# Sturm sweeps of an eigenvalue search: one product of double width and one sum a step on GpSimd in place of three VectorE operations

## The chip, the cores and the metric

The kernel runs on one core of a Trainium2 chip. The metric is the time of one execution on the device in microseconds; lower is better. Several executions are run and their median is given. Besides, one execution is recorded by the hardware profiler; the profile and the trace are of that one.

A core has TensorE (PE: matrix products, with PEld for its weight loads), VectorE (DVE), ScalarE (ACT), GpSimd (POOL) and SyncE (SP, which issues transfers here). Each engine carries out its own queue of instructions in the order in which they were written; the engines wait for each other through semaphores.

## The reference

The program is a network of four graph layers on an input of 128 batches x 64 nodes x 256 features, with an adjacency matrix of 64 x 64. Each layer normalises its input, applies a graph operation and adds the result:

- Layer 0: two graph products with `adj`, then LSTMs over windows of 1, 2, 3 and 4 nodes, whose last states replace nodes.
- Layer 1: a product with a Laplacian that is scaled by the largest eigenvalue, then attention and a two-stage network with normalisations.
- Layer 2: graph attention.
- Layer 3: a product with the eigenvectors of a normalised Laplacian, a small network, and the product back:

```python
L_norm = d_inv_sqrt[:, None] * L * d_inv_sqrt[None, :]
_, U = jnp.linalg.eigh(L_norm)
agg = jnp.einsum('mn,bnd->bmd', U.T, features)
```

So the kernel has to decompose one symmetric 64 x 64 matrix into eigenvalues and eigenvectors. The result is needed only in layer 3, but it is a long chain of small operations.

## The kernel before, in words

**The tiling.** The rows (batch and node) are cut into 64 tiles of 128. Layer 0 works on eight groups of eight tiles; layers 1 to 3 work on sixteen groups of four. Layer 0 is mostly matrix products of 128 x 256 outputs on TensorE, with sigmoids and tanhs on ScalarE and the gate products on VectorE. Some products of windows are made by sums of pieces beforehand, and these sums and the small steps of the normalisations are on GpSimd.

**The eigenvalue search** (`eig_decomp`, line 347) runs beside layer 0. It (1) brings the matrix to tridiagonal form by 62 reflections, (2) finds all 64 eigenvalues by nine sweeps, (3) finds the vectors of the tridiagonal matrix, and (4) puts vectors of degenerate values right and hands the matrices `Ub` and `UTb` to layer 3. All of its small tiles lie in one tile named `arena`, which becomes part of the pool of working buffers once the search is over.

**A sweep** (the loop over `s_`, line 634) tests seven points in the interval of each eigenvalue. Each of 64 partitions holds one eigenvalue, and three variants of the matrix are treated at once, so an operation of the recurrence has 64 partitions x 21 columns. With `D` the diagonal, `E2` the squared couplings and `x` the points, the recurrence is p(k+1) = (D(k) - x) p(k) - E2(k-1) p(k-1), and the number of changes of sign along k tells how many eigenvalues lie below x. `DX` holds D - x for all k, `PL` the values p, and `SG` their signs. For each k, VectorE makes two products and a difference. After every eight steps the last two p are divided by the larger of their sizes, in four VectorE operations: the reduction, a lower bound, the reciprocal, the product. This happens seven times a sweep. At the end of a sweep the signs are compared, the changes are summed over k, and the intervals are shortened eightfold.

**The order of work** is computed when the program is built, by a planner (class `Plan`). Every operation is recorded with what it depends on; `schedule` then writes all queues down, in the order in which a model of the engines would start the operations. It charges each operation a duration by `cost` (line 176), for example

```python
else:
    c = 0.075 + 0.00105 * n          # VectorE, n columns
...
c = 0.44 + 0.14 * n if op.kw.get("op") is ALU.pow else 0.12 + 0.00218 * n   # GpSimd
return c, c + 0.05
```

The second value is the time after which another operation may use the result. The planner lets two kinds of operations never overlap: those of GpSimd, and those of VectorE whose operands all lie in SBUF (`op.port`; reductions and the statistics of normalisations are excepted). Where both could start at one time, VectorE goes first. The search is the group `EIG`: on TensorE its operations go ahead of all others, and on all other engines they go behind all others that could start at that time (`rank`, line 328). On the chip, an engine then waits at the head of its queue for whatever that instruction needs, also where the plan had it ready.

Of the kernel before, what the change touches and what calls it, by code (L numbers as in the profile page):

```python
# [8 lines left out]
ALU = mybir.AluOpType  # L9
# [3 lines left out]
N = 64  # L13
KS = 7
# [332 lines left out]
def eig_decomp(plan, room, adj, adjT, ident, idf, ones):  # L347
# [13 lines left out]
    V, G, PE, ACT, SP = (plan.proxy(e) for e in ("V", "G", "PE", "ACT", "SP"))  # L361
# [3 lines left out]
    def scope():  # L365
        inner.reset([0])
        return inner

    def T(shape, name):
        return room.tile(shape)  # L370

    def W(shape, name, bufs=None):

        if bufs is None:
            bufs = 2 if shape[-1] < N or name == "lab" else 1
        ring = kept.setdefault((name, tuple(shape)), [])
        if len(ring) < bufs:
            ring.append(room.tile(shape))
        else:
            ring.append(ring.pop(0))  # L380
        return ring[-1]
# [56 lines left out]
    ph = scope()  # L438
# [4 lines left out]
    for k in range(N - 2):  # L443
# [17 lines left out]
        s = W([N, 1], 's')  # L461
# [21 lines left out]
        p = pf[:N, :2 * N]  # L483
# [43 lines left out]
    M = N - 1  # L527
# [68 lines left out]
    E2 = T([N, 3, N], 'E2')  # L596
# [30 lines left out]
    V.tensor_copy(lo, l1.to_broadcast([N, 3]))  # L627
    C = 3 * KS
    ph = scope()
    PL = ph.tile([N, N + 1, C])  # L630
    V.memset(PL[:, 0, :], 1.0)
    DX = ph.tile([N, N, 3, KS])
    SG = ph.tile([N, N + 1, C])
    for s_ in range(NSWEEP):
        V.tensor_scalar(w, w, 1.0 / (KS + 1), None, op0=ALU.mult)
        x = W([N, 3, KS], 'x')
        V.tensor_scalar(x, c['ramp'], w, None, op0=ALU.mult)
        V.tensor_add(x, x, lo.unsqueeze(2).to_broadcast([N, 3, KS]))
        for l in range(3):
            V.tensor_mul(DX[:, :, l, :], BM[:, l, :].unsqueeze(2).to_broadcast([N, N, KS]), x[:, l, :].unsqueeze(1).to_broadcast([N, N, KS]))  # L640
            V.tensor_sub(DX[:, :, l, :], DM[:, l, :].unsqueeze(2).to_broadcast([N, N, KS]), DX[:, :, l, :])
        DXf = DX.rearrange('p k l s -> p k (l s)')
        for k in range(N):
            V.tensor_mul(PL[:, k + 1, :], DXf[:, k, :], PL[:, k, :])
            if k:
                b = W([N, 3, KS], 'b', 2)
                V.tensor_mul(b, PL[:, k - 1, :].rearrange('p (l s) -> p l s', l=3), E2[:, :, k - 1:k].to_broadcast([N, 3, KS]))
                V.tensor_sub(PL[:, k + 1, :], PL[:, k + 1, :], b.rearrange('p l s -> p (l s)'))
            if k % 8 == 7 and k < N - 1:
                mm = W([N, C], 'mm')  # L650
                V.tensor_reduce(mm, PL[:, k:k + 2, :].rearrange('p k c -> p c k'), op=ALU.max, axis=AX.X, apply_absolute_value=True)
                V.tensor_scalar(mm, mm, 1e-30, None, op0=ALU.max)
                V.reciprocal(mm, mm)
                V.tensor_mul(PL[:, k:k + 2, :], PL[:, k:k + 2, :], mm.unsqueeze(1).to_broadcast([N, 2, C]))
        V.tensor_scalar(SG, PL, 0.0, None, op0=ALU.is_lt)
        NE = DXf
        V.tensor_tensor(NE, SG[:, 1:, :], SG[:, :N, :], op=ALU.not_equal)
        ct = W([N, 3, KS], 'ct')
        V.tensor_reduce(ct.rearrange('p l s -> p (l s)'), NE.rearrange('p k c -> p c k'), op=ALU.add, axis=AX.X)
        V.tensor_tensor(ct, ct, li.unsqueeze(2).to_broadcast([N, 3, KS]), op=ALU.is_le)  # L660
        sm = W([N, 3], 'sm')
        V.reduce_sum(sm, ct, axis=AX.X)
        V.scalar_tensor_tensor(lo, sm, w, lo, op0=ALU.mult, op1=ALU.add)
# [7 lines left out]
    ph = scope()  # L671
# [80 lines left out]
    def one(name):  # L752
        return W([N, 1], name)
# [7 lines left out]
    for l in (1, 0):  # L761
# [10 lines left out]
        b = one('bc')  # L772
# [11 lines left out]
        t = W([N, N], 't64')  # L784
# [3 lines left out]
        t = W([N, N], 't64')  # L788
# [23 lines left out]
        t = W([N, N], 't64')  # L812
# [120 lines left out]
def gnn_kernel(ctx: ExitStack, tc: tile.TileContext, a, out):  # L933
# [213 lines left out]


    QT, Vc, inner = eig_decomp(plan, room, adj2[:N], adjT2[:N], ident[:N, :N], ident, ones)
    for dst, lhs, rhs in ((Ublk, QT, Vc), (UTblk, Vc, QT)):  # L1150
        l2 = inner.tile([P, 2, N])
# [560 lines left out]
```

## Time and profile before

| what | us |
|---|---|
| median of three runs | 2153.46 (2152.71 to 2155.54) |
| the profiled execution | 2151.09 |
| its span, first to last instruction | 2149.3 |
| TensorE busy | 2102.0 |
| VectorE busy | 1796.7 |
| ScalarE busy | 1124.1 |
| GpSimd busy | 708.4 |
| tridiagonal form and all before it, from the start to | 538 |
| nine sweeps, from and to | 538 to 1178 |
| vectors, from and to | 1178 to 1348 |

The times of the stages are read from the trace: the sweeps begin with the first operations of 64 x 448 and end with the last reduction of 64 x 1344 columns. Almost every instruction stands under line 344, where the planner issues them, so the groups are told apart by the tile names and by the shapes: `arena` is the search, `mids` and `bank` and `big` are the layers. A row of a group gives its count, after the bar its busy time in us and its mean in ns, and then the idle time of the engine before it with what ended it. A row of a timeline gives the start and the length in us. Busy times are of one profiled execution.

### The profile page before, as it was taken

The numbers are of one execution on the slowest core, as the hardware profiler recorded it, in microseconds if no ns is written. First come the engines' busy times: TensorE is split into PE (matmuls) and PEld (weight loads), VectorE is DVE, ScalarE is ACT, GpSimd is POOL, SyncE is SP. The second block draws the span as 40 slices with busy tenths as digits, with TensorE's granted clock in tenths as the row PEclk, the third lists the DMA queues.
The fourth block names the chain that finished last, engine by engine and source line by source line (L and its number), as shares of the span: only waits on it lengthen the run. The fifth ranks groups of instructions, "written<-read, shape, count | busy, mean of one in ns | idle before, by whom it ended". The sixth has DMA issues, their size and how long they took to land.

```text
span 2149.3 us, 46200 instructions
## 1 busy us (share of the span) xinstructions
PE 2102.0 (98%) x16772; PEld 1665.0 (77%) x16772; DVE 1796.7 (84%) x7434; ACT 1124.1 (52%) x2465; POOL 708.4 (33%) x1040
## 2 busy tenths in 40 slices
PE   9999999999999999999999999999999999999998
PEld 6688688688778778778778788877777877887776
DVE  5788888888999999989989898767787789876787
ACT  3354354355345345345345444566667666665783
POOL 7211211310110110110110002696556657864353
PEclk9999999999999999999999999999999999999999
DMA  5000100100100100100000111200000100000001
GB/s 206 1 3 22 42 2 22 41 1 21 40 1 21 40 1 21 40 1 21 26 1 21 50 40 51 90 1 2 21 22 21 41 22 21 11 12 11 2 2 60
DMA packets 44868, 57.70 MB, mean 27 GB/s; under 512 B 8928, under 2 KB 38496, under 8 KB 44640
## 3 DMA queue, kind: packets, MB, share of 16 engines
q1 hardware_dynamic: 43536, 53.71, 7.6%
q8 instruction: 131, 2.15, 0.4%
q10 hardware_dynamic: 1104, 1.05, 0.2%
q14 instruction: 97, 0.79, 0.1%
HBM read 37.53 MB, written 16.78 MB: 25 GB/s over the span
## 4 chain that ended last, share of the span: by engine, by line
PE 79%; DVE 11%; POOL 3%; issue 3%; ACT 2%; DMA 2%; SPq 0%; DVEq 0%; ACTq 0%; POOLq 0%
PE bank L344 79%; DVE stat L344 3%; DVE arena L344 3%; DVE big L344 3%; POOL stat L344 2%; DVE mids L344 1%; DVE sums L344 1%; DMA big<-in_x_dram 1%; ACT big L344 1%; ACT mids L344 1%; POOL arena L344 0%; ACT arena L344 0%; POOL big L344 0%; DVE Whh L344 0%; SPq L344 0%
## 5 line engine op out<-in xcount | busy, mean ns | idle before, releaser
L344 PE MATMUL bank<-big,Wih 128*128 128x256 f32 (+3 forms) x2408 | 731.7, 426 | 14.7 <-DVE arena L344 6.9
L344 PEld LDWEIGHTS bank<-big,Wih 128*128 128x128 f32 x2408 | 440.3, 190 | 183.0 <-issue 100.2
L344 ACT ACTIVATE mids<-bank,bl 128x256 f32<-128x256 f32 (+3 forms) x528 | 274.8, 527 | 385.7 <-PE bank L344 383.3
L344 PE MATMUL bank<-big,Whh 128*128 128x256 f32 (+2 forms) x1692 | 448.0, 366 | 1.5 <-DVE big L344 1.4
L344 DVE TENSOR_TENSOR arena<-arena 64x21 f32<-64x21 f32 (+5 forms) x2253 | 372.3, 195 | 29.5 <-POOL arena L344 1.2
L344 PEld LDWEIGHTS bank<-big,Whh 128*128 128x128 f32 x1692 | 306.8, 190 | 40.6 <-issue 8.6
L344 PE MATMUL bank<-big,sums 128*128 128x168 f32 (+2 forms) x1472 | 263.8, 321 | 1.6 <-ACT big L344 1.5
L344 POOL TENSOR_SCALAR stat<-stat 128x4 f32<-128x4 f32 (+1 forms) x228 | 69.8, 307 | 514.0 <-DVE stat L344 499.2
L344 PEld LDWEIGHTS bank<-big,sums 128*128 128x128 f32 (+1 forms) x1472 | 220.5, 185 | 17.4 <-issue 3.4
L344 ACT COPY mids<-bank 128x168 f32<-128x168 f32 (+2 forms) x427 | 146.2, 364 | 151.9 <-PE bank L344 146.0
L344 DVE TENSOR_TENSOR big<-mids 128x512 f32<-128x512 f32 (+2 forms) x256 | 141.5, 562 | 33.9 <-ACT mids L344 30.7
L344 ACT ACTIVATE mids<-mids,bl 128x336 f32<-128x336 f32 (+3 forms) x192 | 102.1, 539 | 78.7 <-DVE mids L344 74.9
L344 DVE TENSOR_TENSOR mids<-bank,mids 128x168 f32<-128x168 f32 (+2 forms) x322 | 116.1, 368 | 25.1 <-PE bank L344 17.6
L344 DVE SCALAR_TENSOR_TENSOR arena<-arena 64x1 f32<-64x1 f32 (+15 forms) x565 | 124.3, 243 | 6.1 <-POOL arena L344 2.5
L344 POOL TENSOR_TENSOR stat<-stat,mhalf 128x4 f32<-128x4 f32 (+1 forms) x114 | 123.9, 1088 | 5.6
L344 ACT ACTIVATE mids<-big 128x256 f32<-128x256 f32 (+2 forms) x176 | 89.4, 510 | 62.7 <-DVE big L344 46.3
L344 POOL TENSOR_TENSOR big<-big 128x168 f32<-128x168 f32 (+1 forms) x30 | 21.4, 726 | 272.5 <-DVE arena L344 105.7
L344 DVE TENSOR_SCALAR arena<-arena 64x1 f32<-64x1 f32 (+8 forms) x533 | 102.4, 199 | 8.3 <-POOL arena L344 0.4
L344 DVE TENSOR_TENSOR big<-big,mids 128x256 f32<-128x256 f32 (+2 forms) x194 | 95.2, 492 | 9.7 <-ACT mids L344 8.5
L344 PE MATMUL bank<-Wih,big 128*128 128x256 f32 x384 | 94.1, 383 | 3.1 <-DVE big L344 0.9
L344 POOL TENSOR_TENSOR arena<-arena 64x1 f32<-64x1 f32 (+1 forms) x70 | 46.8, 669 | 145.9 <-ACT arena L344 105.8
L344 ACT ACT_TABLE_LOAD x55 | 70.6, 1283 | 35.9 <-PE bank L344 18.0
(371 smaller groups left out, 3747.9 us busy)
## 6 DMA issues: line engine op xcount, KB each, us to landing
big<-in_x_dram SPq DMA_DIRECT2D x30, 512.0 KB, 5.5
put<-big SPq DMA_DIRECT2D x16, 512.0 KB, 2.8
arena<-put SPq DMA_DIRECT2D x8, 512.0 KB, 6.6
out_dram<-arena SPq DMA_DIRECT2D x16, 256.0 KB, 2.3
Wih<-in_WihT_dram SPq DMA_DIRECT2D x3, 1024.0 KB, 11.9
Whh<-in_WhhT_dram SPq DMA_DIRECT2D x3, 1024.0 KB, 13.9
big<-put SPq DMA_DIRECT2D x5, 512.0 KB, 5.4
out_dram<-big SPq DMA_DIRECT2D x10, 256.0 KB, 2.2
```

Source lines behind the costliest of these rows:

```text
L344: getattr(self.engines[op.eng], name)(*map(real, args), **{k: real(a) for k, a in kw.items()})
```

## The change

Each step of the recurrence becomes two GpSimd operations. The coefficients are laid out as pairs, `CO[:, k] = (-E2(k-1), D(k) - x)`, so that one product of 42 columns with the pair (p(k-1), p(k)) makes both terms, and one sum of 21 columns makes p(k+1). The negated couplings are written once, ahead of the sweeps. The first step has one product and stays on VectorE. The row of ones at the head of `PL` is set by GpSimd in each sweep, because the signs now overwrite `PL` and the tile `SG` is gone. The rescale after every eight steps stays on VectorE, with its four operations.

```diff
     PL = ph.tile([N, N + 1, C])
-    V.memset(PL[:, 0, :], 1.0)
-    DX = ph.tile([N, N, 3, KS])
-    SG = ph.tile([N, N + 1, C])
+    CO = ph.tile([N, N, 2, C])
+    l3 = lambda t: t.rearrange('p k (l s) -> p k l s', l=3)
+    DX = l3(CO[:, :, 1, :])
+    for l in range(3):
+        V.tensor_scalar(l3(CO[:, 1:, 0, :])[:, :, l, :], E2[:, l, :M].unsqueeze(2).to_broadcast([N, M, KS]), -1.0, None, op0=ALU.mult)
     for s_ in range(NSWEEP):
...
-        DXf = DX.rearrange('p k l s -> p k (l s)')
-        for k in range(N):
-            V.tensor_mul(PL[:, k + 1, :], DXf[:, k, :], PL[:, k, :])
-            if k:
-                b = W([N, 3, KS], 'b', 2)
-                V.tensor_mul(b, PL[:, k - 1, :].rearrange('p (l s) -> p l s', l=3), E2[:, :, k - 1:k].to_broadcast([N, 3, KS]))
-                V.tensor_sub(PL[:, k + 1, :], PL[:, k + 1, :], b.rearrange('p l s -> p (l s)'))
+        G.memset(PL[:, 0, :], 1.0)
+        V.tensor_mul(PL[:, 1, :], CO[:, 0, 1, :], PL[:, 0, :])
+        for k in range(1, N):
+            b = W([N, 2, C], 'b', 2)
+            G.tensor_tensor(b, PL[:, k - 1:k + 1, :], CO[:, k], op=ALU.mult)
+            G.tensor_tensor(PL[:, k + 1, :], b[:, 0, :], b[:, 1, :], op=ALU.add)
             if k % 8 == 7 and k < N - 1:
...
-        V.tensor_scalar(SG, PL, 0.0, None, op0=ALU.is_lt)
-        NE = DXf
-        V.tensor_tensor(NE, SG[:, 1:, :], SG[:, :N, :], op=ALU.not_equal)
+        V.tensor_scalar(PL, PL, 0.0, None, op0=ALU.is_lt)
+        NE = CO[:, :, 1, :]
+        V.tensor_tensor(NE, PL[:, 1:, :], PL[:, :N, :], op=ALU.not_equal)
```

## The prediction

> **What bounds the kernel now.** I read the page from the top: the span and the busy shares, the 40 slices, then the chain.
>
> ```profile
> span 2149.3 us, 46200 instructions
> PE 2102.0 (98%) x16772; PEld 1665.0 (77%) x16772; DVE 1796.7 (84%) x7434; ACT 1124.1 (52%) x2465; POOL 708.4 (33%) x1040
> PE   9999999999999999999999999999999999999998
> POOL 7211211310110110110110002696556657864353
> PE 79%; DVE 11%; POOL 3%; issue 3%; ACT 2%; DMA 2%; SPq 0%; DVEq 0%; ACTq 0%; POOLq 0%
> ```
>
> TensorE bounds it: busy 2102 of 2149.3 us, in every slice, with 79% of the chain. At most 47 us can be won by taking waits away. GpSimd is nearly empty where the sweeps are. The timeline of VectorE shows the first sweep's operations from 538 us and the last count at 1175 to 1178 us, so nine sweeps take 640 us, 71 each. The sums of that stretch:
>
> ```profile
> 538.00:1178.00 640.00, 633.70 (x3819) 497.86 (x3818) 588.83 (x2697) 285.72 (x647) 67.13 (x96) 1.00 0.06 20
> ```
>
> The columns are the length, then busy PE, weight loads, DVE, ACT and POOL. TensorE idles 6.3 us of 640: the LSTM's matmuls fill it while VectorE, 92% busy, does their elementwise work and the sweeps in between. The sweeps are background work; relief of VectorE alone can win about those 6.3 us, plus some of the 6.2 us in the 170 after.
>
> The groups of that stretch show what goes and what the new owner does for its operations:
>
> ```profile
> L344 DVE TENSOR_TENSOR arena<-arena 64x21 f32<-64x21 f32 x1726 | 241.8, 178 | 17.0
> L344 POOL TENSOR_TENSOR big<-big,big 128x168 f32<-128x168 f32 x24 | 13.8, 606 | 4.0 <-DVE arena L344 3.1 <-DVE big L344 0.8
> L344 POOL TENSOR_SCALAR stat<-stat 128x4 f32<-128x4 f32 x16 | 5.8, 363 | 340.2 <-DVE stat L344 339.2
> ```
>
> GpSimd's timeline in one normalisation shows short operations that depend on each other, and VectorE's one rescale:
>
> ```profile
> 728.06 0.23 POOL L344 TENSOR_SCALAR stat<-stat 128x4 f32<-128x4 f32 x1 [96.30 <-DVE stat L344]
> 728.37 1.04 POOL L344 TENSOR_TENSOR stat<-stat,mhalf 128x4 f32<-128x4 f32 x1
> ...
> 732.34 0.21 POOL L344 TENSOR_TENSOR stat<-stat 128x4 f32<-128x4 f32 x1
> 732.64 0.23 POOL L344 TENSOR_SCALAR stat<-stat 128x4 f32<-128x4 f32 x1
> ```
>
> ```profile
> 546.90 0.19 DVE L344 TENSOR_REDUCE arena<-arena 64x21 f32<-64x42 f32 x1
> 547.13 0.17 DVE L344 TENSOR_SCALAR arena<-arena 64x21 f32<-64x21 f32 x1
> 547.33 0.28 DVE L344 RECIPROCAL arena<-arena 64x21 f32<-64x21 f32 x1
> 547.65 0.91 DVE L344 TENSOR_TENSOR arena<-arena 64x42 f32<-64x42 f32 x6
> ```
>
> A GpSimd product of 4 columns takes 0.21 us, and the next dependent one starts 0.08 to 0.09 us after its end (728.29 to 728.37, 732.55 to 732.64). On VectorE eight 21-wide operations in a row took 1.20 us (from 545.67), 0.15 each.
>
> **What the Trainium skill says.** GPSIMD Engine Reference, section 3.1: a two-input elementwise operation costs GpSimd about 2.6 cycles an element against VectorE's 1. The trace agrees: 128x4 to 128x168 is 0.21 to 0.61 us, 2.4 ns a column. SBUF — State Buffer, section "Who interferes with whom": a VectorE operation with two SBUF inputs and a GpSimd operation that reads SBUF exclude each other for the whole instruction. It agrees: the 128x4 scalar operation, 230 ns at its shortest, has a mean of 363 in this stretch, where such VectorE work, its groups added up, is 82% of the time. Perfetto Trace Analysis, section "GPSIMD Engine Instruction": time GpSimd by the spacing of starts; I do, with the gaps.
>
> **What the change removes, adds and moves.** Each sweep loses 64+126-1 = 189 VectorE operations of 21 columns, 1701 in all: 238 us of 178 ns that overlap in part. Each gains 63 GpSimd products of 42 columns and 63 sums of 21, 1134 in all. The negated couplings (three 441-column operations once, about 0.4 us each by the 64x448 row's 622 ns) and the sign test in place are worth about 1 us on VectorE, hidden under TensorE's 98%; uncovered they cost that 1 us. The nine GpSimd memsets, about 0.1 us each, come at a sweep's start; VectorE's first product waits for them, and what is queued behind it is LSTM products. No DMA moves. What matters is that the recurrence crosses to another engine and back at seven rescales a sweep, in queues whose order is fixed beforehand.
>
> That order is computed with the planner's charges (its cost function). It charges GpSimd 0.12 + 0.00218n us, with 0.05 more of latency, of which 0.04 count on the same engine: 0.212 + 0.166 + 0.08 = 0.457 us a step. The chip's, an estimate: 42 columns 0.28 us and 21 columns 0.24 us, by the 0.208 at 4 columns and the single 128x32 sum's 252 ns, and 0.08 behind each: **0.68 us a step**. Nothing in the trace shows these shapes on 64 partitions, so I bound the step: 0.50 (no gap, 0.26 + 0.24) to 0.95 (every operation met by the lock at the 363/230 ratio, 0.82, and a crossing more).
>
> One sweep on the chip: 63 x 0.68 = 42.8; seven rescales, 0.96 us from 546.90 to 547.86 and two crossings of 0.1, 8.1; ends (sign test, count, new points: 604.53 to 618.98 in the trace) 14.4; GpSimd's other work in its queue, 67.1 us in 640, 6.8 in 65; the lock, 133 ns at 82% share, so 39 ns at the 24% that the LSTM alone has (155 us of such products in 640, its groups added up), times 126, 5.0. Sum 77.1, times nine **694 us**.
>
> One sweep in the written order: 63 x 0.457 = 28.8; rescales by its charges 7 x 1.1 = 7.7; ends 14.4. It lets VectorE's SBUF work and GpSimd never overlap, and VectorE wins ties. The other such work is charged 189 us in 640, 30% (311 VectorE operations 132, 96 GpSimd ones 57), so the chain's 28.8 to 36.5 us stretch by 1/0.7: 12 to 16 more. Sum 63.2 to 66.5, nine **569 to 599 us**; I take 590. TensorE's work beside the sweeps is thus only 590 us worth.
>
> The difference is 104 us. Where it goes: the reduction of each rescale stands in VectorE's in-order queue and waits for GpSimd. Behind it stand the LSTM's gate products, for them ACT's tanh waits, and TensorE's next step for the hidden state. Slack in that chain absorbs a lag once, some us, not 72 times; blocks of eight steps that fit badly add about as much. Finishing the search earlier in TensorE's terms may give back 3 of the 6 us idle after 1178. So 2149.3 + 101 = 2250; the median of the runs stands 4.2 above the profiled span (its execution took 2151.1), so **2254 us**.
>
> **Rivals.**
> Likeliest, chance 0.60: GpSimd's chain paces the sweeps, 2195 to 2320, for steps of about 0.58 to 0.78 us.
> Fits in, 0.12 (0.09 faster): the step costs no more than the order gives it, 0.68 - (694 - 590)/567 = 0.50 us, the lower bound. TensorE then stays the bound and VectorE's relief takes away the waits in and after the sweeps: 2153.5 - 12 = 2142. For it: the planner's charge for 512 columns (1.24 us) meets the 1.15 to 1.33 of the rows, and spans of GpSimd are rough. Against: the gaps are starts less ends, seen at each dependent pair. It decides at 0.50 us a step.
> Half absorbed, 0.13: TensorE's queue has enough ready work to swallow half of each lag: 2204. For it, eight banks and two groups under way; against, one in-order VectorE queue for both.
> Locked harder, 0.15: each GpSimd operation waits for whole products of the LSTM, 0.4 to 0.7 us long, and they for it: 0.14 us in place of 0.04 for 126 x 9 operations, 113 more: 2367. For it, 1.05 us for a 0.23 us operation among the 16; against, most are at 0.23.
> That the work doesn't move is no case: the calls name the engine.
>
> **How the numbers follow.** The range 2170 to 2345 holds the first case, the half-absorbed one and about half of the hard lock; it leaves out the faster end and the far tail. About 0.2% is what a measurement of this kernel can tell from no change. Faster 0.09, same 0.03, slower 0.88.
>
> **What would show it.** TensorE's idle time between the first and last sweep rises from 6 to about 100 us, in gaps ended by VectorE's or ACT's products; VectorE idles before 64x42 reductions with GpSimd as releaser, 63 times, some 1 to 2 us each; the sweeps last near 690 us; GpSimd gains about 300 us busy, VectorE loses 240. If a step's start-to-start is near 0.5 us, or TensorE's idle time stays under 20 us, the prediction is wrong; if a step is near 0.9 us, the lock is larger than I take it.

## The result, and the profile after

The changed kernel takes **2203.4 us** (median of four runs, 2201.9 to 2207.3) against 2153.5 before: 1.0233 times the time, 95% interval 1.0219 to 1.0247. It is 50 us slower. The forecast was slower by 100 us, 2254, with a range of 2170 to 2345. The direction and the mechanism were right, the size was twice too large.

The page of the changed kernel: span, busy shares, and the slices of TensorE, VectorE and GpSimd.

```profile
span 2201.2 us, 45704 instructions
PE 2122.2 (96%) x16772; PEld 1668.6 (76%) x16772; DVE 1595.9 (73%) x5735; ACT 1124.5 (51%) x2465; POOL 1014.5 (46%) x2183
PE   9999999999999999899999999999999999999998
DVE  5788888888555556546555788677779779785787
POOL 7211311211654664565555112397466656864453
PE 33%; DVE 12%; POOL 7%; issue 3%; ACT 1%; DMA 1%; DVEq 0%; POOLq 0%; SPq 0%; ACTq 0%
```

VectorE is 201 us less busy and GpSimd 306 us more. The shares of the chain that ended last add up to 57% only, because the following back ends at 949 us. Of the 1252 us that it covers, TensorE has 58%; in the kernel before, the chain from 897 us on, which is as far from its end, has some 71%.

The stretch of the nine sweeps, now 538 to 1229 us, with the columns as before (length, busy PE, weight loads, DVE, ACT, POOL, and then the granted share of TensorE's clock, the DMA share and GB/s), and two slices of 50 us in it:

```profile
538.00:1229.30 691.30, 652.65 (x3832) 502.01 (x3831) 385.85 (x999) 285.63 (x648) 376.24 (x1238) 0.99 0.05 18
550.00:600.00 50.00, 46.24 (x393) 29.20 (x393) 24.21 (x71) 15.72 (x34) 30.64 (x95) 0.93 0.13 43
900.00:950.00 50.00, 43.72 (x386) 27.79 (x386) 30.62 (x75) 15.15 (x32) 24.84 (x73) 0.93 0.13 43
```

The sweeps take 691 us in place of 640, and all of the loss lies there. TensorE idles 38.7 us in them (6.3 before); in the second slice it stands still for 6.3 us of 50 and the granted clock is 0.93. Beside the sweeps stand 3832 matmuls, almost exactly the 3819 that stood beside the 640 us before; counted by the columns that they write, they are 642 us' worth at the pace of before. What follows is as long as it was: the vectors end 174 us after the sweeps (170 before), with 6.7 us of TensorE idle (6.2).

Two groups of that stretch, then its waits (who waited for whom: total, times, longest), those of VectorE first, then all of TensorE's:

```profile
L344 POOL TENSOR_TENSOR arena<-arena 64x42 f32<-64x42 f32 x567 | 170.0, 300 | 224.4 <-DVE arena L344 184.6 <-DVE big L344 1.4
L344 POOL TENSOR_TENSOR arena<-arena 64x21 f32<-64x21 f32 x567 | 139.2, 245 | 44.1
```

```profile
DVE arena L344 <- POOL arena L344: 148.3, 64, 4.8
DVE big L344 <- ACT mids L344: 74.4, 64, 6.6
DVE mids L344 <- PE bank L344: 47.9, 44, 6.9
```

```profile
PE bank L344 <- DVE mids L344: 15.7, 14, 2.0
PE bank L344 <- DVE big L344: 10.7, 9, 2.4
PE bank L344 <- DVE arena L344: 8.8, 2, 5.0
PE bank L344 <- ACT mids L344: 3.3, 2, 2.1
```

VectorE waits 64 times for the recurrence on GpSimd, 2.3 us each: ahead of 56 of the 63 reductions and of eight sign tests at a sweep's end. TensorE in turn waits almost only for VectorE. One wait in VectorE's timeline, with GpSimd's eight steps in front of it and ScalarE behind it:

```profile
641.33 5.30 POOL L344 TENSOR_TENSOR arena<-arena 64x42 f32<-64x42 f32 x16 [2.20 <-DVE arena L344]
```

```profile
644.06 0.33 DVE L344 TENSOR_TENSOR mids<-bank,mids 128x168 f32<-128x168 f32 x1 [1.35 <-PE bank L344]
646.66 0.19 DVE L344 TENSOR_REDUCE arena<-arena 64x21 f32<-64x42 f32 x1 [2.27 <-POOL arena L344]
646.89 0.17 DVE L344 TENSOR_SCALAR arena<-arena 64x21 f32<-64x21 f32 x1
647.10 0.28 DVE L344 RECIPROCAL arena<-arena 64x21 f32<-64x21 f32 x1
647.30 0.26 DVE L344 TENSOR_TENSOR mids<-bank,mids 128x168 f32<-128x168 f32 x1
```

```profile
647.95 0.57 ACT L344 ACTIVATE mids<-mids,bl 128x336 f32<-128x336 f32 x1 [0.81 <-DVE mids L344]
```

Eight steps take 5.30 us, 0.66 each. The reduction of the rescale waits 2.27 us for them. The LSTM's sums, here at 647.30, stand behind it in the queue, and ScalarE waits 0.81 us for them. From product to product, the starts of the trace give a median step of 0.641 us and a mean of 0.737 over the 495 steps without a rescale.

Of the span's 51.9 us, 31.7 are idle time of TensorE and 20.2 are longer busy time. The trace's record of the granted clock can explain most of the second part: within the span it shows half the clock for 37.5 us, 10.2 before, and 27.3 us at half the clock are up to 13.7 us of work lost. The other 6 us or more stay unexplained.

### The profile page after: what moved, and what is told of

Read it like the earlier page. It is cut to its first block, busy times and chain, and to the rows that moved or that the text cites. A ratio compares the mean times of both kernels' runs of the same rounds, so it can differ in the third digit from the quotient of the medians.

```text
span 2201.2 us, 45704 instructions
## 1 busy us (share of the span) xinstructions
PE 2122.2 (96%) x16772; PEld 1668.6 (76%) x16772; DVE 1595.9 (73%) x5735; ACT 1124.5 (51%) x2465; POOL 1014.5 (46%) x2183
## 4 chain that ended last, share of the span: by engine, by line
PE 33%; DVE 12%; POOL 7%; issue 3%; ACT 1%; DMA 1%; DVEq 0%; POOLq 0%; SPq 0%; ACTq 0%
PE bank L344 33%; POOL arena L344 5%; DVE arena L344 4%; DVE big L344 2%; DVE stat L344 2%; DVE mids L344 1%; POOL stat L344 1%; DVE sums L344 1%; ACT big L344 1%; POOL big L344 1%; DVE Whh L344 0%; DMA arena<-put 0%; ACT arena L344 0%; DMA big<-put 0%; DMA Whh<-in_L_b_dram 0%
## 5 line engine op out<-in xcount | busy, mean ns | idle before, releaser
L344 PE MATMUL bank<-big,Wih 128*128 128x256 f32 (+3 forms) x2408 | 743.1, 430 | 36.2 <-DVE mids L344 16.7
L344 POOL TENSOR_TENSOR arena<-arena 64x21 f32<-64x21 f32 (+3 forms) x1204 | 355.8, 296 | 422.4 <-DVE arena L344 231.1
L344 DVE TENSOR_TENSOR big<-mids 128x512 f32<-128x512 f32 (+2 forms) x256 | 149.3, 594 | 75.5 <-ACT mids L344 72.0
L344 ACT ACTIVATE mids<-mids,bl 128x336 f32<-128x336 f32 (+1 forms) x192 | 102.3, 539 | 98.7 <-DVE mids L344 95.2
L344 DVE TENSOR_TENSOR arena<-arena 64x6 f32<-64x6 f32 (+8 forms) x552 | 136.7, 252 | 13.4 <-POOL arena L344 1.4
L344 DVE TENSOR_REDUCE arena<-arena 64x21 f32<-64x42 f32 (+20 forms) x152 | 50.2, 330 | 129.9 <-POOL arena L344 129.2
L344 ACT ACTIVATE mids<-big 128x512 f32<-128x512 f32 (+2 forms) x176 | 89.4, 509 | 83.9 <-DVE big L344 72.5
L344 POOL MEMSET arena<- 64x2 f32 (+6 forms) x81 | 8.7, 112 | 230.8 <-DVE arena L344 230.8
## 6 DMA issues: line engine op xcount, KB each, us to landing
Whh<-in_WhhT_dram SPq DMA_DIRECT2D x3, 1024.0 KB, 13.7
```

The source lines that it names most:

```text
L344: getattr(self.engines[op.eng], name)(*map(real, args), **{k: real(a) for k, a in kw.items()})
```

## The experiments

The theory after the result: every step of the recurrence takes longer on GpSimd than the written order allows it, VectorE's queue waits for the difference at each rescale, and TensorE loses it. Rivals: the hand-overs between the engines, contention for SBUF, slack that swallows part, and a search that simply ends too late.

**1. A shorter step in the same order.** `plan.force` sets the charge (duration, and the time to the use of the result) of the operations that follow it. Here it is what the changed kernel charges, so that all queues keep their order, and the operations are made small. 20 of 21 columns are not computed, so the eigenvalues are not found; one fill of `PL` with ones, charged nothing, stands ahead of the sweeps.

```diff
...
-            G.tensor_tensor(b, PL[:, k - 1:k + 1, :], CO[:, k], op=ALU.mult)
-            G.tensor_tensor(PL[:, k + 1, :], b[:, 0, :], b[:, 1, :], op=ALU.add)
+            plan.force = (0.21156, 0.26156)
+            G.tensor_tensor(b[:, :, :1], PL[:, k - 1:k + 1, :1], CO[:, k, :, :1], op=ALU.mult)
+            plan.force = (0.16578, 0.21578)
+            G.tensor_tensor(PL[:, k + 1, :1], b[:, 0, :1], b[:, 1, :1], op=ALU.add)
+            plan.force = None
...
```

> The order of the changed kernel kept, instruction by instruction, but the product works on 2 columns and the sum on 1 (20 of 21 columns are left out; the eigenvalues are then not computed). A step is about 0.08 us shorter. Theory (each 0.01 us of a step costs 5 to 6 us): 2150 to 2170, TensorE's idle time in the sweeps falls below 20 us. Rival (hand-overs at the rescales and contention with VectorE make the loss): above 2190.

Measured: 2158.6 us, ratio 1.003 (1.002 to 1.0039). The mean step is 0.633 us. The stretch of the sweeps:

```profile
538.00:1182.00 644.00, 635.38 (x3818) 498.15 (x3817) 380.02 (x994) 285.05 (x645) 319.03 (x1238) 1.00 0.06 19
```

TensorE idles 8.6 us in 644. All hand-overs, semaphores and queues are still there, and so is what contention with VectorE there may be: the 488 steps with no other GpSimd operation between have a mean 0.07 us above their median, as in the changed kernel. Yet all but 5 of the 50 us are gone. What was lost hangs on the length of the step.

**2. A longer step in the same order.** The product covers 84 columns; the sum uses the first half as before. The buffer `b` is twice as large, and the charges are again those of the changed kernel.

```diff
...
-            G.tensor_tensor(b, PL[:, k - 1:k + 1, :], CO[:, k], op=ALU.mult)
+            m = 2 if k < N - 1 else 1
+            plan.force = (0.21156, 0.26156)
+            G.tensor_tensor(b[:, :2 * m, :], PL[:, k - 1:k - 1 + 2 * m, :], CO[:, k:k + m].rearrange('p a t c -> p (a t) c'), op=ALU.mult)
...
```

> The order of the changed kernel kept, but the product works on 84 columns in place of 42 (the second half is not used): 42 columns more, 0.06 to 0.09 us a step. Theory: 558 steps times that, 33 to 50 us more: 2236 to 2255. Rival (slack swallows part of each lag): under 2225.

Measured: 2244.9 us, 1.0426 (1.041 to 1.0441).

```profile
538.00:1272.00 734.00, 668.35 (x3836) 511.85 (x3836) 389.20 (x1005) 285.88 (x649) 419.98 (x1238) 0.97 0.05 17
```

The mean step rises by 0.081 us (0.737 to 0.818) and the time by 41.5 us: 512 us for each us of a step, where all 558 lengthened steps would give 558. The sweeps grow by 43 us, because the steps with a rescale stay at 2.69 us on average; of these 43 nearly all arrives at the end. Slack swallows next to nothing.

**3. An honest order.** The two operations are charged so that a step takes 0.64 us in the written order.

```diff
...
+            plan.force = (0.30, 0.35)
             G.tensor_tensor(b, PL[:, k - 1:k + 1, :], CO[:, k], op=ALU.mult)
+            plan.force = (0.26, 0.31)
             G.tensor_tensor(PL[:, k + 1, :], b[:, 0, :], b[:, 1, :], op=ALU.add)
+            plan.force = None
...
```

> The changed kernel, but the planner charges the two GpSimd operations of a step 0.30 and 0.26 us, so that a step takes 0.64 us in the written order, as its median on the chip. Theory (the order promised 0.457 us a step and VectorE waits for the rest): the waits go, TensorE idles under 15 us between 538 us and the last sweep, whose length is now the written one; but the search then ends about 110 us later than before and layer 3 waits for it, so 2210 to 2245. Rival (only the order is at fault, the search has room): 2145 to 2160.

Measured: 2245.5 us, 1.0429 (1.0414 to 1.0445), slower still and at the upper end of the expected range. The first row is the sweeps, the second the vectors:

```profile
538.00:1285.00 747.00, 736.61 (x4321) 577.81 (x4320) 419.01 (x1086) 329.84 (x742) 380.02 (x1254) 1.00 0.07 23
1285.00:1475.00 190.00, 135.57 (x803) 111.57 (x806) 152.23 (x679) 59.25 (x127) 34.37 (x51) 0.83 0.12 40
```

In the sweeps TensorE now idles only 10.4 us: the order is true and 4321 matmuls stand beside it. But the sweeps last 747 us, the search ends at 1475, and TensorE idles 54 us in the second stretch, where it had 6. A true order moves the bill from the sweeps to the end; it pays only if the search still ends in time.

**4. Is there room at the end?** The kernel before, with one sweep more.

```diff
-NSWEEP = 9
+NSWEEP = 10
```

> The kernel before, all on VectorE, with ten sweeps in place of nine (one more refinement). Theory (the search ends just in time before, so any search longer by one sweep of 65 to 75 us makes layer 3 wait, also where the order is true): 2190 to 2215, with TensorE idle after 1350 us and not in the sweeps. Rival (the search is background work with room to spare): 2150 to 2160.

Measured: 2208.2 us, 1.0256 (1.024 to 1.0271).

```profile
538.00:1241.00 703.00, 695.57 (x4130) 544.12 (x4129) 644.76 (x2976) 309.75 (x696) 72.41 (x104) 1.00 0.07 22
1241.00:1438.00 197.00, 158.79 (x876) 132.98 (x874) 158.17 (x700) 74.51 (x163) 36.42 (x55) 0.89 0.15 48
```

63 us more of search cost 55, all of it after the sweeps (38 us idle in place of 6, and a granted clock of 0.89). TensorE waits 32 us longer there, so at most 31 of the 63 us were to spare before the change. That is a deadline, which my prediction had not seen: I had called it background work.

**5. A search that ends earlier, the order as in the change.** The changed kernel with eight sweeps; the last refinement is left out.

```diff
-NSWEEP = 9
+NSWEEP = 8
```

> The changed kernel with eight sweeps in place of nine (the last eightfold refinement of the eigenvalues is left out); the search then ends some 75 us earlier. Theory (the loss is paid sweep by sweep inside the LSTM stage): eight ninths of the 50 us stay, 2193 to 2202. Rival (the search ends too late for layer 3, and that alone costs the 50 us): 2150 to 2158.

Measured: 2190.6 us, 1.0174 (1.0159 to 1.0189), just below the expected range.

```profile
538.00:1150.00 612.00, 576.67 (x3456) 440.49 (x3455) 341.75 (x884) 246.68 (x556) 333.69 (x1103) 0.99 0.06 19
```

The search ends at 1315 us, earlier than before the change, and 37 of the 50 us are still lost; TensorE idles 35.3 us in the sweeps. So in the changed kernel the deadline isn't what costs. Eight ninths would have been 44. The sweeps last 612 us and the matmuls beside them, by columns, are 574 us' worth, so the 37 us are again the sweeps' own; why they are fewer than 44 is open.

**6. Fewer hand-overs.** Three rescales a sweep in place of seven.

```diff
-            if k % 8 == 7 and k < N - 1:
+            if k % 16 == 15 and k < N - 1:
```

> The changed kernel with a rescale after every 16 steps, three a sweep in place of seven. The search's written end moves about 75 us forward, the step charges stay. Theory (each of the 567 steps is 0.12 us longer than written, and that is the loss): 2198 to 2212, although the search then ends early. Rival (the hand-overs to VectorE and back make the loss, 0.8 us each): four ninths to less of it is left, 2165 to 2185.

Measured: 2205.1 us, 1.024 (1.0226 to 1.0254), the same as the change.

```profile
538.00:1163.00 625.00, 579.42 (x3437) 441.43 (x3435) 329.95 (x774) 245.12 (x552) 364.53 (x1230) 0.97 0.06 18
```

36 of 63 rescales are gone, the sweeps last 625 us, and TensorE idles 45.6 us in them. The hand-overs are not the loss.

**7. The arithmetic without the engine.** The product of double width and the sum, on VectorE.

```diff
-            G.tensor_tensor(b, PL[:, k - 1:k + 1, :], CO[:, k], op=ALU.mult)
-            G.tensor_tensor(PL[:, k + 1, :], b[:, 0, :], b[:, 1, :], op=ALU.add)
+            V.tensor_tensor(b, PL[:, k - 1:k + 1, :], CO[:, k], op=ALU.mult)
+            V.tensor_tensor(PL[:, k + 1, :], b[:, 0, :], b[:, 1, :], op=ALU.add)
```

> The changed kernel's arithmetic, the product of double width and the sum, but both on VectorE as the operations before were. Theory (the form of the arithmetic is free, the loss is GpSimd's step against the written one): no loss, 2148 to 2156, since TensorE fills the time anyway; VectorE is about 85 us less busy than before. Rival (the double-width layout or the in-place signs cost time by themselves): 2175 or more.

Measured: 2153.8 us, 1.0002 (0.9994 to 1.001): no difference. The form of the arithmetic, the in-place signs and the new layout cost nothing. VectorE's busy time fell by 18 us only, not by 85, with 565 fewer instructions. An operation of 42 columns takes 202 ns and one of 21 columns 183. In the trace before, two starts of 21-column operations in a row mostly lie 0.09 to 0.11 us apart or 0.21, the short distance about twice as often, which fits two products and a difference that needs them; with the pair, where each operation needs the one ahead, nearly every distance is 0.21 or 0.23.

**8. The term that the forecast lacked.** On VectorE the search goes ahead of the LSTM in the written order.

```diff
-            return (-2 if op.eng == "PE" else 1000, op.index)
+            return (-2 if op.eng in ("PE", "V") else 1000, op.index)
```

> The changed kernel, but on VectorE the search's operations go ahead of the LSTM's in the written order, as they do on TensorE. Theory (my sums left out that at each rescale and sweep end the search stands behind the LSTM on VectorE): from the last product before a rescale to the next product 2.69 us fall to 1.7 to 2.1, the nine sweeps to 620 to 650 us, and fewer matmuls than 3832 stand beside them, 3500 to 3650; the loss by the steps stays, and the LSTM waits a little: 2200 to 2225. Rival (the rescale is long by its own four operations and the hand-overs): the 2.69 us stay within 0.2.

Measured: 2211.5 us, 1.0273 (1.0258 to 1.0289). The sweeps begin at 517 us:

```profile
517.00:1161.40 644.40, 604.95 (x3568) 466.57 (x3567) 357.23 (x941) 255.13 (x579) 371.07 (x1230) 0.98 0.06 19
```

From the last product before a rescale to the next product it is 2.13 us in place of 2.69 (a little over the expected range), and 3568 matmuls stand beside the sweeps in place of 3832. At the pace of before (640 us for 3819) that is 598 us of TensorE's work in place of 642; by columns it is 594. The sweeps on the chip are shorter by about as much, 644 us in place of 691, so the lag stays at 46 to 50 us and the loss does not shrink. It is even 8 us larger, and about 7 of them lie ahead of the sweeps: at 517 us TensorE has done 3229 matmuls, 3271 in the kernel before.

**9. The rule that keeps the two engines apart.** The honest charges of experiment 3, but the planner lets the two operations overlap VectorE's work in SBUF.

```diff
-        op.port = eng == "G" or (eng == "V" and ...
+        op.port = eng == "G" and not self.force or (eng == "V" and ...
```

> As the honest order, 0.64 us a step, but without the planner's rule that GpSimd's two operations never overlap VectorE's SBUF work. Theory (that rule, not the charges, made the honest order's sweeps 84 us long): sweeps of 74 to 80 us, the search ends 1395 to 1435, 2185 to 2215. Rival (on the chip the two engines block each other as the rule says): sweeps of 83 or more, 2235 or more.

Measured: 2199.7 us, 1.0222 (1.0205 to 1.0239).

```profile
538.00:1217.00 679.00, 662.83 (x3930) 519.14 (x3929) 392.55 (x1018) 291.76 (x663) 373.00 (x1238) 1.00 0.06 18
```

The sweeps last 679 us, 75 each, in place of 83, and the search ends at 1410. So 68 of the 747 us of experiment 3's sweeps came from that rule. It asks for more than the chip does: over the 488 steps of the changed kernel with no other GpSimd operation between, the mean is 0.709 us against a median of 0.64, which leaves at most 0.069 us a step for contention with VectorE.

**10. A true order that ends in time.** Three rescales, no exclusion, and charges for 0.72 us a step, its mean with contention.

```diff
-        op.port = eng == "G" or (eng == "V" and ...
+        op.port = eng == "G" and not self.force or (eng == "V" and ...
...
+            plan.force = (0.34, 0.39)
             G.tensor_tensor(b, PL[:, k - 1:k + 1, :], CO[:, k], op=ALU.mult)
+            plan.force = (0.3, 0.35)
             G.tensor_tensor(PL[:, k + 1, :], b[:, 0, :], b[:, 1, :], op=ALU.add)
-            if k % 8 == 7 and k < N - 1:
+            plan.force = None
+            if k % 16 == 15 and k < N - 1:
```

> The changed kernel with three rescales a sweep, the two operations charged so that a step takes 0.72 us in the written order (its mean on the chip with contention), and without the planner's rule that they never overlap VectorE's SBUF work. The written search then ends near 1354 us, as before. Theory (order true and search in time): no loss, 2148 to 2162, TensorE idle under 12 us in the sweeps. Rival (GpSimd beside VectorE costs the LSTM time in itself): 2180 or more.

Measured: 2164.0 us, 1.005 (1.0037 to 1.0063), 2 us above the expected range.

```profile
538.00:1191.00 653.00, 643.16 (x3840) 502.89 (x3839) 368.90 (x873) 286.94 (x651) 378.06 (x1238) 0.99 0.06 19
```

39 of the 50 us are gone with the recurrence still on GpSimd, and TensorE idles 9.8 us in the sweeps. The rest is in its busy time, which is 11 us longer than before; the record shows half the clock for 32.7 us in place of 10.2, which is worth up to 11.2. Three edits are made at once here, so what each is worth alone is not shown. None of these versions beats the kernel before: TensorE's 2102 us of work leave 47 us, and none of the edits reaches them.

**The runs side by side.** For every run whose search ends in time, the sweeps' length less the TensorE work that stands beside them (their matmuls by columns, at the pace of before) can be set against the loss:

| run | sweeps, us | work beside them, us | difference | loss, us |
|---|---|---|---|---|
| the change | 691 | 642 | 49 | 50 |
| 1, shorter step | 644 | 639 | 5 | 5 |
| 2, longer step | 734 | 643 | 91 | 91 |
| 5, eight sweeps | 612 | 574 | 38 | 37 |
| 6, three rescales | 625 | 570 | 55 | 52 |
| 8, search first | 644 | 594 | 50 | 58 |
| 10, true and short | 653 | 644 | 9 | 11 |

## Why the prediction was right and wrong

**The bound and where a loss would show: right.** TensorE's idle time in the sweeps rose from 6 to 39 us (100 were forecast), VectorE idled with GpSimd as releaser before 56 of the 63 reductions, 2.3 us each (1 to 2 were forecast), and the sweeps last 691 us (694). Experiments 1 and 2 show that the step's length is the cause.

**The chip's sweep, 77.1 us: right, nearly term by term.** The starts in the trace give 55 steps of 0.737, seven of 2.69 at the rescales, and 17.9 us from the last product of a sweep to the first of the next: 77.3. To compare it with the sum, GpSimd's other work has to be taken out of all three. It stands in seven of the 495 steps, in seven of the 63 rescales (7.5 us each, the other 56 take 2.09) and in three of the eight sweep ends (22.7 us, the other five 15.0). Then a sweep's steps are 39.0 us (41.7 were forecast, the lock included), its rescales 14.7 (13.4), its end 15.0 (15.2), and what the other work adds is 8.6 (6.8). That the lock's 0.079 us a step comes near the most that it can be, 0.069, has some luck in it: the mean of 363 ns that it came from was made by five of the 16 operations, at 546 ns or more, while the other eleven took 230 to 267.

**The sweep in the written order: wrong, and this is the step that failed.** "Sum 63.2 to 66.5, nine 569 to 599 us; I take 590. TensorE's work beside the sweeps is thus only 590 us worth." 3832 matmuls stand there, as many as before in 640 us: 642 us' worth, so the order's sweep is about 71 us and not 65.5. The sum lacked the search's place behind the layers' work. At a rescale and at a sweep's end the order lets ready work of the layers pass on VectorE and GpSimd, and where there is much of it, as in a normalisation, that is several us. For the chip I had a term for such work, 6.8 us a sweep on GpSimd. For the order I had the rescales' own charges, 7 x 1.1, the ends, and a stretch by shares of time. Experiment 8 puts the search ahead on VectorE, and the work beside the sweeps falls to 594 to 598 us, inside the 569 to 599 of my sum. The term is worth 44 to 48 us. It lengthens the chip's sweeps as well, by 47, so it is no loss by itself; the forecast was too large because it stood on one side of the difference only. The lag is not the 104 us that I had but 691 - 642 = 49, which is the loss.

The planner's own start times say the same. They are no measurement: `schedule` gives one to each operation when the changed kernel is built. Its nine sweeps last 646 us there. The same distances, on the chip and in the written order:

| from one product to the next | times | chip, us | order, us |
|---|---|---|---|
| step, nothing between | 488 | 0.709 | 0.578 |
| step, other GpSimd work between | 7 | 2.7 | 3.2 |
| rescale, nothing between | 56 | 2.09 | 2.15 |
| rescale, other GpSimd work between | 7 | 7.5 | 8.8 |
| sweep end, nothing between | 5 | 15.0 | 15.5 |
| sweep end, other GpSimd work between | 3 | 22.7 | 23.2 |

Only the plain step takes longer on the chip than the order gives it, 0.131 us, and 488 of them make 64 us; all else is a little shorter and gives some 20 us back. My 0.50 us, the step at which nothing would be lost, was too low as well: at a mean step of 0.633 experiment 1 still loses 5 us, and a line through it and the changed kernel reaches no loss at about 0.62 (an estimate from the two). The order's mean step is 0.615.

**The rivals.** "Fits in" fell: the order gives a plain step 0.58 us on average, the chip takes 0.71. "Half absorbed" named 2204 us, nearly the result, by a mechanism that isn't there: nearly all of an added lag passes through (experiment 2). "Locked harder", 0.14 us an operation, fell: it is 0.034 at most. The 3 us that I wanted back after 1178 didn't come.

**What I had not asked** is whether the search has a deadline. "Background work" was true of its rank, but before the change it ended with at most 31 us to spare (experiment 4). So the obvious repair, honest charges, made things worse (experiment 3), and a repair needs both a true order and a shorter chain (experiment 10). That an honest order with room takes most of the loss away is shown. That the rest, 11 us, is the clock's is likely from the record of the clock but not shown, and nothing here was faster than before.

## What to carry to other kernels

When queues are written down beforehand, the cost of a moved operation is the difference between its time on the chip and the time that the order gave it, once for each instance in a chain; so work out the order's side with the same care as the chip's, including every place where the moved work stands behind other work. What stands in the way on both sides, in the order and on the chip, is no loss and must be in both sums or in neither. In this kernel a lag in VectorE's in-order queue, on which all layers depend, passed through almost whole, though VectorE was busy for 73% of the span and GpSimd for 46%. Before correcting the order, ask when the chain must end: here the background work had at most 31 us to spare.

## What the runs showed of the hardware

- TensorE's clock. In the changed kernel the record shows half the clock for 3.4 or 6.8 us after stretches in which TensorE was only partly idle: in the 3.4 us ahead of the six such spells between 230 and 1520 us it was busy for a share of 0.07 to 0.52. Five of the six follow a single gap of 1.6 to 5.0 us, one follows two of 1.1 and 0.6. Waits of TensorE thus cost twice in these runs, once as idle time and once as slower matmuls after it: in experiment 3, with 102 us at half the clock, its busy time was 33 us longer than before for the same work (2135.1 against 2102.0).
- Short dependent GpSimd operations on 64 partitions: a product of 42 columns takes 265 ns in the median and a sum of 21 columns 217, with 0.08 us between them. Of a step of 0.641 us, the 63 columns' own share is small: with 2 columns and 1 column the medians are 191 and 183 ns, and the step is still 0.531 us. A product of 84 columns takes 354 ns, so a column adds about 2 ns.
- A VectorE operation of 42 columns (202 ns) costs hardly more than one of 21 (183 ns).
